# Six pipeline steps of the next tree issued beside the last leaf tiles of q and k, and overfull leaves in buffers of their own

## Chip, cores and metric

The kernel runs on one core of one Trainium2 chip. The metric is the device time of one execution in microseconds (us); lower is better. Before the change the median of 14 executions is 2463.23 us (2460.74 to 2474.45).

The engines are named as in the profile: PE (matrix multiply, with PEld its weight loads), DVE (vector), ACT (scalar, which also issues DMAs), POOL (GpSimd, which here issues all indirect DMAs) and SP (which only issues DMAs). Each runs its own instruction stream in order, and they meet through semaphores.

## What is computed

The input is 4 x 1024 tokens of 256 numbers. Three residual blocks follow one another: half of a fast-feedforward attention block, a 16-head attention block, and the feedforward block once more.

```python
x = x + 0.5 * ffn(layernorm(x), ...)
x = x + attention(layernorm(x), ...)
x = x + 0.5 * ffn(layernorm(x), ...)
```

Inside `ffn` there are four hard-routed trees, q, k, v and f. A tree walks 8 levels for each token (`node = 2*node + 1 + (logit > 0)`), arrives at one of 256 leaves, and applies that leaf's two small layers (256 to 16 and 16 to 256):

```python
h = act(einsum('bsd,bsdl->bsl', x, w1[leaf]) + b1[leaf])
return einsum('bsl,bsld->bsd', h, w2[leaf]) + b2[leaf]
```

q, k and v are trees over the same normalised rows, then `softmax(q k^T / 16) v` is added, and the f tree (gelu in place of relu) runs over the result.

## The kernel before, in words

**Leaf tiles.** The first five levels of a tree are one matrix product for all tokens; they give each token one of 32 blocks of eight leaves. Tokens are sorted by block into tiles of 128 rows, every tile belonging to one block. There are 48 tiles that are always computed and, where blocks fill badly, up to 15 more: `SPARE = (0, 48, 53, 58, NGRP)` (L294) cuts them into parts.

**The pipeline of a tree** is the generator `leaves` (L827). A tile passes five stages: `load` gathers its rows by an indirect DMA on POOL (L819), `turn` transposes them on PE (L844) and copies them on ACT (L846), `hidden` is the first layer and the last three levels (PE L866 and L873, DVE L882 to L897), `active` transposes that (PE L911, L912; ACT L920, L923), and `result` is the second layer (PE L931, L932), a copy (ACT L946) and a store to DRAM (SP L947). Step g of the loop runs the result of tile g-6, `hidden` of g-2, `turn` of g, `active` of g-4, and asks for the rows of g+4. So the 48 tiles take 54 steps, of which the first six fill the pipeline and the last six drain it. The rings of buffers: five for gathered rows, three each for most others. The first three tiles of k and v have rows of their own (`first_rows`, L1080).

**Beside the leaves.** `with_steps` (L1056) calls one step of each side generator after each step of the main one: the placement of the next tree's tokens (`placing`, about 42 steps, whose product `inv` the next gathers need and whose `gblk` names each tile's block), in the first `ffn` the building of the next tree's first layer from raw weights (`load_first`, 16 pieces, one every third step) and the keeping of this one in DRAM (`keep_first`). In the second `ffn` the first layer is loaded back in one DMA instead (`load_kept`, 4352 KB).

**Spare tiles.** After the 54 steps of a tree, `spare_leaves` (L809) runs the parts above 48 in three nested conditional blocks. The number of tiles used is loaded into a register of each engine (L797), and each engine branches by itself (L811). A skipped block must still bring the semaphores to the counts that it would have reached, so each engine waits at the branch for its own outstanding work: PE, DVE and ACT for theirs, POOL for its gathers and SP for the DMAs of the SP and ACT queues. Nothing outside a conditional block is mixed with what is inside, so the blocks also part the program.

**Order.** The leaves of q, k and v are not in an order written by hand: when the program is built, the instructions between two conditional blocks are put into an order for each engine by priority (program order) and by a plan of when each is ready. Instructions marked `keep_in_program_order` keep theirs.

**Between trees.** In the loop over q and k (L1176) the next tree's weights are asked for at the top: biases, second layer and, in the first `ffn`, raw weights, from the ACT queue. The tiles of v share their buffers with q's weights, so those loads wait for the last tile of q, spare ones included. Behind the loop v's leaves run beside `coming` (L1230), which gathers 24 finished k and q tiles from DRAM on POOL and transposes them for the scores (L1227), one every second step.

Of the kernel before, what the change touches and what calls it, by code (L numbers as in the profile page):

```python
# [77 lines left out]
def macaron_kernel(ctx: ExitStack, tc: tile.TileContext, a: dict, out: bass.AP):  # L78
# [223 lines left out]
    def split_b2(pool):  # L302

        n = NBLK // B2G * E
        rest = pool.tile([P, n], F32, name="b2_rest")
        part = [pool.tile([P, n], BF16, name=f"b2_part{s}") for s in range(3)]
        none = pool.tile([P, 3 * B2P // P], BF16, name="b2_none")
        nc.gpsimd.memset(none, 0.0)
        for f, nm in enumerate(FFFS):
            nc.scalar.dma_start(  # L310
                rest[f * NBLK : (f + 1) * NBLK].rearrange("p (q c) -> p q c", c=E),
                a[f"{nm}_b2"].rearrange("(q p) c -> p q c", p=NBLK),
            )
            nc.gpsimd.dma_start(
                b2i[f].rearrange("s n -> (s n)").rearrange("(p c) -> p c", p=P), none
            )
        for s in range(3):
            nc.gpsimd.tensor_copy(part[s], rest)
            for f in range(len(FFFS)):
                rows = b2i[f][s].rearrange("(r n) -> r n", r=B2G)[:, : EPB * B2W]  # L320
                nc.gpsimd.dma_start(
                    rows.rearrange("r (e w) -> r e w", e=EPB)[:, :, :n],
                    part[s][f * NBLK : (f + 1) * NBLK],
                )
            if s < 2:
                nc.gpsimd.tensor_sub(rest, rest, part[s])

# [467 lines left out]
    def tiles_used(gblk):  # L795
# [11 lines left out]
        return used  # L807

    def spare_leaves(used, *what):  # L809

# [216 lines left out]
    def ffn(first: bool, last: bool):  # L1027
# [6 lines left out]
        def stage(es, name, bufs, side="left"):  # L1034
            return es.enter_context(
                tc.tile_pool(name=name, bufs=bufs, side=side, reuse_waits="tile")
            )

        with ExitStack() as es:
# [31 lines left out]
            with ExitStack() as ws, banks(0, 8):  # L1071
                wp = stage(ws, "w", 1)

                fp = stage(ws, "first", 1)

                def tree(lp, f, got, *weights):
                    what = b1p[f], sel[f], own[f], inv[f], gblk[f], AF.Relu, None, got
                    return lp, f, *weights, *what

                def first_rows(f):  # L1080
# [3 lines left out]
                with ExitStack() as hs, ExitStack() as rs:  # L1084
                    hot = hots_of(stage(hs, "hots", 1), 3)
                    raw = stage(hs, "raw", 1) if first else None

# [84 lines left out]
                    wb = stage(rs, "w_k", 1, "right")  # L1172
                    lp = stage(hs, "leaves", 2)
                    pp = stage(hs, "place", 1)
                    got = {}
                    for f in range(2):  # L1176
                        what = tree(lp, f, got, w1, w2, b2s)
                        used = tiles_used(gblk[f])
# [19 lines left out]
                        else:  # L1198
                            tc.keep_in_program_order(load_kept(nc.scalar, f + 1, w1))
                            sides = ((1, second(10)),)  # L1200
                        with_steps(leaves(*what), (1, placing(pp, f + 1)[1]()), *sides)
                        (w2,) = coming_w2
                        got = first_rows(f + 1)
                        spare_leaves(used, *what)
                    if first:
# [3 lines left out]
                hold_rows()  # L1209
                lp = stage(ws, "leaves_v", 2)  # L1210
                early = stage(ws, "early", 2)
# [36 lines left out]

                what = tree(lp, 2, got, w1, w2, b2s)
                used = tiles_used(gblk[2])  # L1250
                sides = ((1, keep_first(2, w1, 4, 4, 4, 4)),) if first else ()
                with_steps(leaves(*what), (1, coming()), *sides)
                spare_leaves(used, *what)

# [661 lines left out]
```

## Time and profile before

| | us |
|---|---|
| median of 14 runs | 2463.23 |
| the profiled execution, its own time | 2469.78 |
| its span, first to last instruction | 2468.0 |
| leaf tiles of q, k, v in the first ffn, first transposes | 121.2, 228.9, 326.0 |
| leaf tiles of q, k, v in the second ffn, first transposes | 1737.3, 1844.8, 1945.8 |
| tiles of q, k, v in the first ffn | 48, 48, 53 |
| tiles of q, k, v in the second ffn | 53, 48, 48 |

The profiled execution lies 6.55 us above the median. Times in the profile are counted from the start of the span. A row of the timeline gives start, duration, engine, source line, operation, the tile it writes and reads, and in brackets how long the engine was idle before and what ended that; "issue" means that the engine waited for nothing that the profile shows. The granted clock (PEclk) is PE's clock as the throttle gave it, as a share of full speed.

### The profile page before, as it was taken

How to read it: one execution, taken by the hardware profiler on the slowest of the kernel's cores; microseconds unless marked ns; L12 is line 12 of the kernel's file. 1: busy time of each engine (PE TensorE's matmuls, PEld its weight loads, DVE VectorE, ACT ScalarE, POOL GpSimd, SP SyncE). 2: the span in 40 equal slices, each digit the busy share in tenths (PEclk: the TensorE clock that was granted, in tenths of full speed). 3: DMA queues.
4: the chain of work that ended last, by engine and by line, in shares of the span. 5: the costliest groups of instructions: out<-in, count | busy, mean ns of one | idle time of the engine just before them, and what ended most of it. 6: DMA issues, size and time to landing. Idle time of an engine off the chain costs nothing. (4 is left out here: it accounts for less than half of the span.)

```text
span 2468.0 us, 42918 instructions
## 1 busy us (share of the span) xinstructions
PE 2171.6 (88%) x13949; PEld 1391.3 (56%) x13949; DVE 1419.9 (58%) x4712; ACT 1076.4 (44%) x2870; POOL 814.0 (33%) x1045
## 2 busy tenths in 40 slices
PE   4588979999997889999999999995788889999794
PEld 2377867666666644434434444433677776666483
DVE  6676745333346766666676667746757553333475
ACT  3255546233323324555555555553455562332142
POOL 4554546332244521101100100001545563432553
PEclk8699989999998889999999999998899999999897
DMA  9687776343355400000000000008557564431655
GB/s 322 197 277 239 251 238 167 128 120 120 101 182 183 142 1 1 1 1 1 1 14 6 1 10 16 12 8 306 180 154 251 158 173 152 126 107 39 201 163 166
DMA packets 201876, 303.34 MB, mean 123 GB/s; under 512 B 25130, under 2 KB 174011, under 8 KB 197025
## 3 DMA queue, kind: packets, MB, share of 16 engines
q1 hardware_dynamic: 104080, 112.89, 14.1%
q0 software_dynamic: 35552, 91.87, 13.1%
q10 hardware_dynamic: 62000, 95.52, 11.3%
q8 instruction: 130, 2.13, 0.4%
q14 instruction: 114, 0.93, 0.1%
HBM read 182.88 MB, written 122.15 MB: 124 GB/s over the span
## 5 line engine op out<-in xcount | busy, mean ns | idle before, releaser
L1666 DVE TENSOR_REDUCE mxh<-big 128x1 f32<-128x512 f32 (+3 forms) x768 | 393.0, 552 | 194.1 <-PE big L1658 192.3
L1702 ACT ACTIVATE pTh<-big 128x512 f32<-128x512 f32 (+3 forms) x768 | 341.3, 491 | 288.9 <-PE big L1658 265.0
L1658 PE MATMUL big<-kTh,qTh 32*128 32x512 f32 (+3 forms) x1536 | 402.0, 538 | 1.5 <-ACT kTh L1639 1.4
L1694 PE MATMUL big<-qTh,kTh 32*128 32x512 f32 (+3 forms) x1536 | 400.7, 537 | 1.9 <-ACT pTh L1702 1.6
L846 ACT COPY xgT<-sm 128x256 f32<-128x256 f32 x399 | 148.6, 373 | 292.2 <-PE sm L844 258.9
L995 PE MATMUL two<-kT,qT 128*128 128x512 f32 x512 | 234.3, 602 | 9.7 <-issue 8.3
L1023 PE MATMUL sm<-vb,pT 128*128 128x256 f32 x1024 | 232.6, 380 | 0.0
L1694 PEld LDWEIGHTS big<-qTh,kTh 32*128 32x128 f32 x1536 | 143.5, 184 | 156.6 <-issue 127.0
L1023 PEld LDWEIGHTS sm<-vb,pT 128*128 128x128 f32 x1024 | 189.7, 190 | 24.6 <-issue 1.0
L844 PE MATMUL sm<-ident,xg 128*128 128x128 f32 x774 | 157.2, 287 | 41.2 <-DMA xg<-xs_f 11.9
L1003 DVE TENSOR_REDUCE mx<-two 128x1 f32<-128x1024 f32 x64 | 78.3, 1224 | 195.1 <-PE two L995 195.1
L882 DVE SCALAR_TENSOR_TENSOR went<-sm,sides 128x14 bf16<-128x14 f32 x399 | 67.9, 170 | 181.0 <-PE sm L873 171.9
L1713 PE MATMUL sm<-pTh,vpad 128*32 128x512 f32 (+3 forms) x1536 | 165.2, 501 | 0.0
L1658 PEld LDWEIGHTS big<-kTh,qTh 32*128 32x128 f32 x1536 | 146.4, 185 | 20.3 <-issue 14.1
L995 PEld LDWEIGHTS two<-kT,qT 128*128 128x128 f32 x512 | 93.7, 192 | 107.3 <-issue 104.0
L946 ACT COPY og<-sm 128x256 f32<-128x256 f32 x298 | 111.0, 373 | 90.2 <-DMA os_q<-og 21.3
L819 POOL DMA_INDIRECT xg<-rows_x,inv_q x101 | 101.5, 1005 | 112.2 <-PE sm L912 50.6
L937 POOL DMA_INDIRECT ytok<-og,tok x101 | 99.3, 983 | 80.5 <-DVE went L882 68.0
L420 POOL TENSOR_TENSOR acc<-acc,oh 128x32 bf16<-128x32 bf16 (+1 forms) x128 | 39.6, 310 | 253.0 <-DVE oh L418 221.9
L819 POOL DMA_INDIRECT xg<-rows_x,inv_k x90 | 91.9, 1021 | 89.8 <-PE sm L912 46.8
L897 DVE TENSOR_TENSOR hm<-sm,mask 128x128 f32<-128x128 f32 x399 | 115.2, 289 | 10.1
L920 ACT ACTIVATE hid<-sm 128x128 f32<-128x128 f32 x399 | 112.9, 283 | 10.6 <-PE sm L912 10.4
(371 smaller groups left out, 4417.2 us busy)
## 6 DMA issues: line engine op xcount, KB each, us to landing
xs_f<-zero ACTq DMA_DIRECT2D x14, 1028.0 KB
xg<-xs_f SPq DMA_DIRECT2D x101, 128.5 KB
os_q<-og SPq DMA_DIRECT2D x101, 128.0 KB
os_v<-og SPq DMA_DIRECT2D x101, 128.0 KB
os_k<-og SPq DMA_DIRECT2D x96, 128.0 KB
xn<-in_x SPq DMA_DIRECT2D x16, 512.0 KB
w_q<-in_q_w SPq DMA_DIRECT2D x2, 4096.0 KB
rows_x<-xn ACTq DMA_DIRECT2D x16, 512.0 KB
```

What stands on the lines that cost most here:

```text
L819: nc.gpsimd.indirect_dma_start(out=xg, out_offset=None, in_=rows_x, in_offset=bass.IndirectOffsetOnAxis(ap=inv[:, g : g + 1], axis=0),)
L844: nc.tensor.transpose(pa[:, c, :], xg[:, c * P : (c + 1) * P], ident)
L846: nc.scalar.copy(xT, pa)
L897: nc.vector.tensor_tensor(hm.rearrange("p (e l) -> p e l", l=LW), ph[:, :P].rearrange(split, l=LW), bc(mask[:, 0], 2, LW), ALU.mult,)
L920: nc.scalar.activation(hid, pt[:, 0], func)
L995: nc.tensor.matmul(ps[:, n0 : n0 + 512], qT[:, c, i * P : (i + 1) * P], kT[:, c, n0 : n0 + 512], start=(c == 0), stop=(c == KC - 1),)
L1023: nc.tensor.matmul(po, pT[:, j, :], vb[:, j, :], start=(j == 0), stop=(j == TPB - 1))
L1658: matmul = nc.tensor.matmul(ps[:, :n], qT[r : r + HPAD, hg, i * P : (i + 1) * P], kT[r : r + HPAD, hg, n0 : n0 + n], start=True, stop=True,)
L1666: nc.vector.tensor_reduce(maxima(b, hg)[:, i, c, u : u + 1], ps[:, :n], AX.X, ALU.max)
L1694: matmul = nc.tensor.matmul(ps[:, off:], kT[r : r + HPAD, hg, j * P : (j + 1) * P], qT[r : r + HPAD, hg, qb * QN + off : (qb + 1) * QN], s ...
L1702: nc.scalar.activation(pT[:, u, off:], ps[:, off:], AF.Exp, scale=1.0 / math.sqrt(HD))
L1713: nc.tensor.matmul(acc[r : r + HPAD, off:], vpads[b % 2][:, j, 4 * hg + 2 * pair + u, :], pTs[pair][:, u, off:], start=(j == 0), stop=(j = ...
```

## The change

The loop no longer makes a new `leaves` generator for each tree. One generator `main` is carried along. A side generator `head` waits for 44 steps, gathers the next tree's first rows, waits for four more, makes the next tree's generator and runs its first six steps; the next turn of the loop, or v's part, goes on from there with 48 steps left. The spare tiles come after these six steps, so in q and k they can't use the rings in which the next tree's tiles now wait: `Carved` cuts rings for them from the two 8 KB buffers for raw weights. These buffers now exist in the second `ffn` too, and the pool of leaf buffers is opened at the start of the `ffn` and kept through v. To make room, `split_b2` holds two of its three parts at a time and fills `b2i` from a zero buffer half as large.

```diff
-        part = [pool.tile([P, n], BF16, name=f"b2_part{s}") for s in range(3)]
-        none = pool.tile([P, 3 * B2P // P], BF16, name="b2_none")
+        none = pool.tile([P, 3 * B2P // P // 2], BF16, name="b2_none")
...
         for s in range(3):
-            nc.gpsimd.tensor_copy(part[s], rest)
+            part = pool.tile([P, n], BF16, name=f"b2_part{s}", tag="b2_part", bufs=2)
+            nc.gpsimd.tensor_copy(part, rest)
...
+    class Carved:
+
+        RINGS = {
+            "xg": (0, 0, 5, E), "hm": (0, 5 * E, 3, P), "hid": (0, 5 * E + 3 * P, 3, P),
+            "xgT": (1, 0, 3, E), "mask": (1, 3 * E, 4, B2R // 2),
+            "mT": (1, 3 * E + 2 * B2R, 3, P // 2),
+        }
+
+        def __init__(self, pool, raw):
+            self.pool, self.turn = pool, {}
+            self.homes = [
+                raw.tile([P, P * LW], F32, name=f"carved{i}", tag="raw", bufs=2)
+                for i in range(2)
+            ]
+
+        def tile(self, shape, dtype, name, tag, bufs=None):
+            if tag not in self.RINGS:
+                return self.pool.tile(shape, dtype, name=name, tag=tag, bufs=bufs)
+            home, at, n, width = self.RINGS[tag]
+            k = self.turn[tag] = (self.turn.get(tag, -1) + 1) % n
+            rows = self.homes[home][: shape[0], at + k * width : at + (k + 1) * width]
...
                 fp = stage(ws, "first", 1)
+                lp = stage(ws, "leaves", 2)
...
+                HEAD = 6
...
-                    raw = stage(hs, "raw", 1) if first else None
+                    raw = stage(hs, "raw", 1)
...
-                    lp = stage(hs, "leaves", 2)
                     pp = stage(hs, "place", 1)
-                    got = {}
+                    main = leaves(*tree(lp, 0, {}, w1, w2, b2s))
+
+                    def head(f, weights):
+
+                        nonlocal main
+                        for _ in range(SPARE[1] - PRE):
+                            yield
+                        rows = first_rows(f)
+                        for _ in range(PRE):
+                            yield
+                        main = leaves(*tree(lp, f, rows, *weights()))
+                        yield from islice(main, HEAD)
+
                     for f in range(2):
-                        what = tree(lp, f, got, w1, w2, b2s)
+                        spare = w1, w2, b2s
...
-                        with_steps(leaves(*what), (1, placing(pp, f + 1)[1]()), *sides)
+                        with_steps(
+                            main,
+                            (1, placing(pp, f + 1)[1]()),
+                            *sides,
+                            (1, head(f + 1, lambda: (w1, coming_w2[0], b2s))),
+                        )
                         (w2,) = coming_w2
-                        got = first_rows(f + 1)
-                        spare_leaves(used, *what)
+                        spare_leaves(used, *tree(Carved(lp, raw), f, {}, *spare))
...
-                lp = stage(ws, "leaves_v", 2)
...
-                what = tree(lp, 2, got, w1, w2, b2s)
                 used = tiles_used(gblk[2])
                 sides = ((1, keep_first(2, w1, 4, 4, 4, 4)),) if first else ()
-                with_steps(leaves(*what), (1, coming()), *sides)
-                spare_leaves(used, *what)
+                with_steps(main, (1, coming()), *sides)
+                spare_leaves(used, *tree(lp, 2, {}, w1, w2, b2s))
```

More of the change, by code (lines that the diff above doesn't have):

```diff
@@ L314, in split_b2 @@
             nc.gpsimd.dma_start(
-                b2i[f].rearrange("s n -> (s n)").rearrange("(p c) -> p c", p=P), none
+                b2i[f].rearrange("s n -> (s n)").rearrange("(p i c) -> p i c", p=P, i=2),
+                bc(none, 1, 2),
             )
         for s in range(3):
-            nc.gpsimd.tensor_copy(part[s], rest)
+            part = pool.tile([P, n], BF16, name=f"b2_part{s}", tag="b2_part", bufs=2)
+            nc.gpsimd.tensor_copy(part, rest)
             for f in range(len(FFFS)):
@@ L322, in split_b2 @@
                     rows.rearrange("r (e w) -> r e w", e=EPB)[:, :, :n],
-                    part[s][f * NBLK : (f + 1) * NBLK],
+                    part[f * NBLK : (f + 1) * NBLK],
                 )
             if s < 2:
-                nc.gpsimd.tensor_sub(rest, rest, part[s])
+                nc.gpsimd.tensor_sub(rest, rest, part)
     def clear(queue, rows):
@@ L807, in tiles_used @@
         return used
+    class Carved:
[16 more added lines that the diff above has]
+            rows = self.homes[home][: shape[0], at + k * width : at + (k + 1) * width]
+            if dtype != F32:
+                rows = rows.bitcast(dtype)
+            if len(shape) == 3:
+                rows = rows.rearrange("p (a b) -> p a b", b=shape[2])
+            return rows
     def spare_leaves(used, *what):
```

## The prediction

> **What bounds the kernel now.** I read the page first, then the timeline of PE around the four places where q hands over to k and k to v, then POOL, ACT and SP there, then the waits in v.
>
> ```profile
> span 2468.0 us, 42918 instructions
> PE 2171.6 (88%) x13949; PEld 1391.3 (56%) x13949; DVE 1419.9 (58%) x4712; ACT 1076.4 (44%) x2870; POOL 814.0 (33%) x1045
> ```
>
> PE is busy 88% of the span, so its gaps are what can be won. Inside the leaf tiles there are few:
>
> ```profile
> 1814.09 0.65 PE L931 MATMUL sm<-w_q,hid 128*128 x2
> ...
> 1815.60 0.65 PE L931 MATMUL sm<-w_q,hid 128*128 x2
> ...
> 223.81 0.28 PE L932 MATMUL sm<-b2s_q,mT 96*128 x1
> 228.86 0.66 PE L844 MATMUL sm<-ident,xf 128*128 128x128 f32 x2 [4.78 <-issue]
> ```
>
> A full step takes 1.51 us (first two rows). The last two rows are the hand-over of q to k in the first ffn: PE ends q, and for 4.78 us waits for nothing that the profile shows, while it jumps over the skipped spare block (the branches of L811 in PE's queue last up to 5.63 us). The other three gaps are 3.95 (322.1), 4.74 (1840.1, after q's five spare tiles) and 6.18 us (1939.6), on the mean 4.91. From the last full step of one tree to the first result of the next:
>
> ```profile
> 217.46:236.37 18.91, 12.02 (x78) 9.71 (x76) 8.36 (x42) 6.35 (x21) 7.70 (x11) 0.82 0.83 247
> 317.52:336.10 18.58, 11.58 (x68) 9.77 (x66) 5.46 (x24) 5.48 (x18) 2.45 (x4) 0.72 0.57 178
> 1822.76:1853.17 30.41, 21.15 (x130) 16.87 (x128) 12.30 (x60) 10.43 (x36) 5.06 (x7) 0.83 0.56 155
> 1935.10:1953.71 18.61, 11.78 (x66) 9.92 (x65) 5.54 (x24) 5.40 (x18) 9.06 (x10) 0.72 0.44 131
> ```
>
> The columns are the length, then busy time of PE, PEld, DVE, ACT and POOL, the granted clock, the DMA share and GB/s. I call these T1 to T4. In T1, T2 and T4 some 18.7 us pass for six steps of work, 6 x 1.51 = 9.06. Half of the bubble is drain and fill, half the jump.
>
> **The change, part by part.** Drain and fill become six full steps, 9.06 us. The jump stays: the branch still stands between six steps and the rest, and its code is still there: 4.91 us. The load of 16 block numbers into PE's registers moves into the full steps; where it stands between full steps now (292.1, 1911.8) it costs 1.21 and 0.52 us, so 0.87. And PE comes out of the jump slow:
>
> ```profile
> 229.00:233.00 4.00, 3.75 (x18) 3.11 (x19) 2.69 (x12) 1.12 (x3) 2.66 (x5) 0.51 1.10 311
> 1948.00:1953.00 5.00, 5.00 (x26) 4.76 (x25) 2.91 (x13) 1.30 (x4) 3.87 (x4) 0.50 0.60 197
> ```
>
> Four us at 0.51 lose 4 x 0.49 = 2.0 us of full steps, where before they hid in a half-empty fill. So a clean hand-over takes 9.06 + 0.87 + 4.91 + 2.0 = 16.8 us.
>
> [...]
>
> T1: 18.91 becomes 16.8, a gain of 2.1. But the carved rings take both raw buffers at the branch, so the first two raw_v loads, now issued at 194.6 and 216.7, move behind it on ACT's queue (0.34 us each to issue), ahead of the copies for PE, and must wait until POOL too has passed its branch. PE's first turn of raw_v comes two slow steps after the jump, some 6 us, about what 1 MB takes to land; I charge 0.6. T1 gains 1.5; bounds: a gain of 8.5 if the jump shrinks to almost nothing, a loss of 3 if raw_v comes late.
>
> T2: here the new tree's first layer is built by 16 pieces, every third step, and k's generator has only 48 steps left, so the last piece now falls into k's drain. v's first layer waits for it; drain (4.6) plus two pieces (0.7 each), four fill steps of about 1.2, jump, registers and slow clock make 4.6 + 1.4 + 4.8 + 4.9 + 0.9 + 2.0 = 18.6, as long as now. What T2 does win is a later stall (2.86 us at 341.8, v's gathers queued on POOL behind gathers of k's results, which waited for SP's branch at 334.0). v is bound by POOL:
>
> ```profile
> 2022.42 0.95 POOL L819 DMA_INDIRECT xg<-rows_x,inv_v  x1 [0.30 <-PE sm L912]
> 2023.67 0.95 POOL L982 DMA_INDIRECT y_k<-os_k,slot_k  x1 [0.30 <-PE sm L873]
> 2024.92 0.95 POOL L982 DMA_INDIRECT y_k<-os_k,slot_k  x1 [0.30 <-PE sm L932]
> ```
>
> One gather each 1.25 us, 72 for v's 48 tiles and 24 fetched ones. Seven of v's tiles are gathered before the branches now, ten afterwards: 3 x 1.25 = 3.75. I take 3.5; bounds a gain of 7 and a loss of 1.
>
> T4 has no build: 18.61 becomes 16.8, 1.8, of which POOL leaves, by the same count, about 1.2; bounds 3.5 and a loss of 1.5.
>
> T3 holds q's spare tiles and v's weights:
>
> ```profile
> 1840.46 0.94 POOL L819 DMA_INDIRECT xg<-rows_x,inv_k  x1 [17.53 <-PEq L811]
> 1847.01 0.44 ACTq L788 DMA_DIRECT2D w_v<-w1d_v  x1
> 1853.01 0.94 POOL L819 DMA_INDIRECT xg<-rows_x,inv_k  x1 [6.60 <-PE sm L873]
> 1863.33 0.66 PE L844 MATMUL sm<-ident,xg 128*128 128x128 f32 x2 [5.85 <-DMA xg<-rows_x,inv_k]
> ```
>
> k's gathers wait for the end of q's spare tiles, then run into the 4352 KB load of w_v (issued at 1847.0), and PE stands 5.85 us for tile 8. In the new order q's drain and k's fill end at 1822.8 + 9.9 = 1832.7. The spare gathers, now queued behind k's ten on POOL, come some 3 us late (a gather lands 2.7 to 4.8 us after its issue where no weights load); five spare tiles then take 10 us as now (1830.3 to 1840.1), to 1845.5, 5.4 later than now. So the weight load also starts 5.4 later and again holds a gather up, to about 1868, but at tile 12 instead of 8. Tile 12 is turned at 1872.2 now. I take 3.5; bounds a gain of 5 and a loss of 3.
>
> **A cost behind.** v's generator also has only 48 steps left, and `coming` needs 53. The 24th fetch is called after v's last step, and its buffer is free only once the 21st is turned: the fetch, 3 us to land and the turn may stand at v's end. Between 0 (the plan draws it forward) and 4 us in each ffn; I take 1.5 each, 3.0, since the planner drew POOL's gathers ahead elsewhere (k's first rows at 197.6, before q's last).
>
> **At nothing.** The third b2 part waits for the four DMAs of the first, issued at 34.4 to 36.8, while its copy runs at 49.9: covered by 13 us of POOL's work; without that cover the accumulation of routes (L420), queued behind it, would be late. The zero buffer's memset, 1.53 us, is halved, while POOL is idle for 24 us afterwards. q's first gathers no longer share memory with the placement; they start at 114.1, when the index lies ready at 113.3: 0 to 1 us, counted as 0. The ten gathers issued early go through POOL past nothing that is waited for, as POOL stands idle 5 to 17 us at each hand-over.
>
> **Sum.** -1.5 - 3.5 - 3.5 - 1.2 + 3.0 = -6.7. The profiled execution would go from 2469.78 to 2463.1, the median, 6.55 below it, from 2463.2 to 2456.5; I say **2456**. Its own range, not all terms at one end, is 2448 to 2461. No change is 2458.3 to 2468.2 (0.2%).
>
> **The rivals.** *Half a change.* `head` needs 54 steps and k has 48, so for v the six steps are called after k's drain. If the plan leaves them there, T2 and T4 gain nothing: -1.5 - 3.5 + 3.0 = -2.0, 2461. For it: program order is the priority. Against: the plan does draw work forward (the gathers at 197.6), and k's drain leaves PE idle slots.
>
> *POOL starves PE.* The slower side, one mechanism. POOL must pass its own skip before k's tile 10 is gathered:
>
> ```profile
> 314.51 0.94 POOL L819 DMA_INDIRECT xg<-rows_x,inv_v  x1 [5.05 <-DMA xg<-rows_x,inv_k]
> ```
>
> That skip waited 5.05 us here, 6.45 at 1935 and from 1821.7 to 1830.7 with the spare tiles, always hidden because PE drained. Now POOL reaches it only after gathering tile 9, about 8.5 us behind the last full step. At 5.5 us for the skip and 4 to land, tile 10 is there at 18; PE comes out of the jump at 14.8 and needs it four tiles, 8 us, later. If the skip takes 9 and the landing 7 (as at 227.6 under a weight load), it comes at 25.5, 2.5 late, with another 1 to 2 us of slow clock. The mechanism decides from 14 us for both together. At 4 us in each of four hand-overs, and the tails at their dearer end (+5): -6.7 + 16 + 5 = +14, 2477; without the tails 2472.
>
> *A short jump.* If PE found its code, T1 to T4 would gain 4 x (4.5 + 2.0) = 26 more: 2430. Neither target nor distance changes, so little speaks for it.
>
> **How the numbers follow.** Forecast 0.55 (faster 0.46, within 0.2% 0.08, slower 0.01); half a change 0.21 (0.03, 0.15, 0.03); starved 0.18 (0, 0.01, 0.17); short jump 0.06 (faster). Faster 0.55, same 0.24, slower 0.21. The range reaches to 2446 (half of the short jump's cases and the best bounds of T1 and T3) and to 2470, where the starved case begins.
>
> **What would show it.** PE: full steps of 1.51 us straight across the last tiles of q and k, then one gap of 4 to 6 us, then slow matmuls of 0.42 for 0.27 us. POOL: ten gathers of the next tree before the skip. PE's wait for gathered rows in T3 still there, four tiles later. Turns of y_k after v's last result would show the tail. Wrong: PE waiting after the jump for gathered rows or for raw_v; drain and fill of T2 and T4 still one after the other.

## The result, and the profile after

The changed kernel takes 2496.63 us (median of 6 runs, 2487.96 to 2498.29) against 2463.23 (28 runs): ratio 1.0123, 95% interval 1.0107 to 1.0139. It is 33 us slower, where 7 us less were forecast. The profiled execution took 2494.32 us, 2.3 below its median; that of before lay 6.55 above its own. So the two traces differ by 24.5 us only, and some 9 us of the medians' difference are in neither.

The top of the page, to be held against the first fence of the prediction:

```profile
span 2492.5 us, 42895 instructions
PE 2174.1 (87%) x13949; PEld 1389.8 (56%) x13949; DVE 1416.8 (57%) x4712; ACT 1073.2 (43%) x2870; POOL 814.2 (33%) x1045
```

PE does the same 13,949 matmuls in 2.5 us more of busy time and idles 22 us longer. The hand-overs themselves, from the last result of one tree to the first of the next (T1 to T4; the third has q's spare tiles in it), and four microseconds behind the last jump, with the columns as before (length; busy PE, PEld, DVE, ACT, POOL; granted clock; DMA share; GB/s):

```profile
219.84:225.55 5.71, 1.42 (x11) 1.09 (x11) 1.18 (x6) 1.17 (x4) 1.56 (x2) 1.00 0.52 146
329.84:341.60 11.76, 5.47 (x43) 4.66 (x42) 4.11 (x18) 3.12 (x10) 1.89 (x2) 0.86 0.69 222
1842.77:1865.19 22.42, 12.64 (x74) 9.82 (x73) 6.54 (x30) 6.83 (x23) 6.66 (x7) 0.77 0.47 87
1960.11:1971.70 11.59, 5.02 (x38) 4.21 (x37) 3.41 (x17) 3.17 (x11) 1.89 (x2) 0.93 0.33 103
1971.00:1975.00 4.00, 4.00 (x16) 3.18 (x16) 1.23 (x5) 0.97 (x3) 1.70 (x2) 0.50 0.20 59
```

So the next tree's first result follows the last one's sooner. But only at q's hand-overs do the six steps stand beside the last tiles. In T1 k's first turns lie among q's last results; in T2 v's first turn comes behind k's last result, and in T4 too (1959.94 after 1959.31):

```profile
215.89 0.38 PE L872 MATMUL sm<-ident,xf 128*128 128x128 f32 x2
...
219.08 0.65 PE L959 MATMUL sm<-w_q,hid 128*128 x2
...
329.03 0.70 PE L959 MATMUL sm<-w_k,hid 128*128 x2
...
330.12 0.60 PE L872 MATMUL sm<-ident,xf 128*128 128x128 f32 x4
```

`head` needs 54 steps and k's generator has 48 left, and the plan did not draw v's steps forward: drain and fill still follow one another there. What T2 and T4 gain is a fill ahead of the jump, at a granted clock of 1.00 (4.7 and 5.3 us to the jump), in place of one behind it, at 0.53 to 0.54 (10.1 and 7.9 us to v's first result).

The time is lost elsewhere. The timeline of PE shows where (start, duration, what is computed, idle time ahead and what ended it):

```profile
225.05 0.67 PE L959 MATMUL sm<-w_k,hid 128*128 x2 [4.29 <-issue]
...
340.62 1.19 PE L959 MATMUL sm<-w_v,hid 128*128 x2 [5.78 <-SPq L839]
...
1749.73 0.66 PE L872 MATMUL sm<-ident,xg 128*128 128x128 f32 x2 [9.22 <-DMA xg<-rows_x,inv_q]
...
1851.01 0.66 PE L872 MATMUL sm<-ident,carved 128*128 128x128 f32 x2 [6.84 <-DMA carved<-rows_x,inv_q]
...
1887.14 1.22 PE L959 MATMUL sm<-w_k,hid 128*128 x2 [10.06 <-ACT hid L948]
...
1970.72 1.19 PE L959 MATMUL sm<-w_v,hid 128*128 x2 [5.52 <-issue]
...
2053.94 0.41 PE L1272 MATMUL sm<-ident,y_k 128*128 128x128 f32 x2 [2.31 <-DMA y_k<-os_k,slot_k]
...
2062.00 4.57 PE L1023 MATMUL two<-kT,qT 128*128 128x512 f32 x6 [5.67 <-issue]
```

The first, second and sixth row are the jump over the skipped block, about as long as before (4.78, 3.95 and 6.18 us there). The third is new: q's second tile in the second `ffn` waits 9.22 us for its rows. The fourth is a spare tile of q that waits for its own. The fifth is the old wait beside the load of w_v, nearly twice as long (10.06 us after 5.85) and now through ACT and the stores. The seventh is the tail: a fetched k row is still to be turned behind v's last result (2051.1), and the eighth is the gap ahead of the scores. ACT's queue has the cause of two of them; first the changed kernel, then the kernel before:

```profile
1734.53 1.27 ACTq L998 DMA_DIRECT2D b2s_k<-b2i_k  x3
1738.49 0.35 ACTq L789 DMA_DIRECT2D w_k<-w1d_k  x1
...
1869.00 0.43 ACTq L789 DMA_DIRECT2D w_v<-w1d_v  x1
...
1886.26 0.37 ACT L974 COPY og<-sm 128x256 f32<-128x256 f32 x1 [12.66 <-DMA os_k<-og]
```

```profile
1708.67 1.60 ACTq L970 DMA_DIRECT2D b2s_k<-b2i_k  x3
1710.32 0.43 ACTq L788 DMA_DIRECT2D w_k<-w1d_k  x1
```

The 4352 KB of w_k were asked for 24 us ahead of q's first gather (1734.41); now they are asked for 1.7 us behind it (1736.80), and the five gathers issued from 1738.2 to 1743.2 take 11.4 to 14.5 us to land, in place of 2.7 to 3.5 for those issued from 1735.8 to 1740.8 before. w_v is asked for at 1869.0, lands at 1885.8, and the stores of k's results issued at 1870 to 1872 land at 1886.2 to 1886.9, so that ACT stands 12.66 us for a result buffer and PE behind it.

The same two traces by stage. "q48" is the 48th result of q, "k24" the 24th of k, and so on; each number is the difference of two such times.

| stage | before | after | difference |
|---|---|---|---|
| start to q1, first `ffn` | 130.8 | 133.2 | +2.5 |
| q1 to k24 (T1 in it) | 150.4 | 148.5 | -1.9 |
| k24 to v48 (T2) | 141.7 | 139.0 | -2.6 |
| v48 to the first scores | 17.3 | 21.9 | +4.6 |
| scores to the end of f | 393.8 | 394.6 | +0.7 |
| end of f to q12, second `ffn` | 933.0 | 942.4 | +9.4 |
| q12 to q48 | 62.9 | 63.3 | +0.5 |
| q48 to k24 (T3) | 73.6 | 80.7 | +7.2 |
| k24 to v48 (T4) | 130.3 | 127.4 | -2.8 |
| v48 to the first scores | 4.7 | 10.9 | +6.2 |
| scores to the end of f | 394.8 | 395.8 | +1.0 |

Three hand-overs gain, 7.3 together. Five other places lose 29.9. The row of T2 is itself a sum: from k24 to k48 the first `ffn` takes 47.9 us in place of 40.7, and from k48 to v48 9.8 less. So from q's first to k's last result, T1 and all of k, it takes 196.6 us in place of 191.3.

### The profile page after: what moved, and what is told of

Its sections match the earlier page's. It is cut to its first block, busy times and chain, and to the rows that moved or that the text cites. A ratio compares the mean times of both kernels' runs of the same rounds, so it can differ in the third digit from the quotient of the medians.

```text
span 2492.5 us, 42895 instructions
## 1 busy us (share of the span) xinstructions
PE 2174.1 (87%) x13949; PEld 1389.8 (56%) x13949; DVE 1416.8 (57%) x4712; ACT 1073.2 (43%) x2870; POOL 814.2 (33%) x1045
## 5 line engine op out<-in xcount | busy, mean ns | idle before, releaser
L1031 DVE TENSOR_REDUCE mx<-two 128x1 f32<-128x1024 f32 x64 | 78.3, 1224 | 197.0 <-PE two L1023 197.0
L910 DVE SCALAR_TENSOR_TENSOR went<-sm,sides 128x14 bf16<-128x14 f32 x399 | 67.7, 170 | 191.3 <-PE sm L901 174.2
L925 DVE TENSOR_TENSOR hm<-sm,mask 128x128 f32<-128x128 f32 x394 | 113.8, 289 | 10.1
L948 ACT ACTIVATE hid<-sm 128x128 f32<-128x128 f32 x394 | 112.0, 284 | 10.4 <-PE sm L940 10.2
```

What stands on the lines that cost most here:

```text
L925: nc.vector.tensor_tensor(hm.rearrange("p (e l) -> p e l", l=LW), ph[:, :P].rearrange(split, l=LW), bc(mask[:, 0], 2, LW), ALU.mult,)
L948: nc.scalar.activation(hid, pt[:, 0], func)
```

## The experiments

My theory after this reading: the bubbles were cover. In them weights were loaded, POOL passed its own branch, and stores drained; without them the same work stands beside running tiles. And two edits that I had counted at nothing (memory, zero buffer) have a price of their own. The rivals stand in the expectations.

Twelve of the fifteen runs were made on chips where the kernel before takes 2570 to 2576 us in place of 2463 to 2467 (v's tiles, f and the scores are slower there, see the end); ratios are to the kernel before on the same chip, and stages are compared between kernels run on like chips.

**b2_alone**: the changed `split_b2` in the kernel before.

> The kernel before with the changed split_b2 alone (two parts at a time, zero buffer half as large). Theory 'small pieces': the zero fill in pieces of half the size takes the DMA engines longer at the very start and delays the input rows; q's first transpose comes at about 123.2 us in place of 121.2, and the whole is 2 us slower, about 2465. Rival 'chance': the 2 us at the start belong to the one profiled execution; 121.2 and 2463 again.

Ratio 1.0018 (0.9996 to 1.0040), 2574.3 against 2569.75. The first transpose of input rows and the zero fills on POOL, in this kernel and then before:

```profile
3.96 0.72 POOL L313 DMA_DIRECT2D b2i_q<-b_none  x1 [0.24 <-POOL b_k L725]
...
5.70 1.09 POOL L313 DMA_DIRECT2D b2i_f<-b_none  x1
...
32.13 2.16 PE L391 MATMUL sm<-ident,xn 128*128 128x128 f32 x8 [7.85 <-ACT xn L1142]
```

```profile
4.67 0.57 POOL L314 DMA_DIRECT2D b2i_q<-b_none  x1 [0.24 <-POOL b_k L724]
...
6.29 0.54 POOL L314 DMA_DIRECT2D b2i_f<-b_none  x1
...
30.18 2.17 PE L390 MATMUL sm<-ident,xn 128*128 128x128 f32 x8 [7.85 <-ACT xn L1141]
```

The fills start 0.6 to 0.7 us earlier, and the rows still come 1.95 us later. Over all traces of this study, the row on PE comes at 30.2 to 31.4 in the four with pieces of the old size and at 31.9 to 33.8 in the thirteen with halves: 2.4 us on the mean, of which 1.5 are left at q's first transpose (121.3 against 122.8, with single traces from 120.2 to 122.8 and from 120.5 to 124.3). The total alone could not show it.

**carved_alone, no_head, own_rings_2nd**: which edit moved w_k's load.

The first is made from the kernel before (for q and k; `Carved` is added), the others from the changed kernel, in this order:

```diff
-  raw = stage(hs, "raw", 1) if first else None
+  raw = stage(hs, "raw", 1)
...
-  spare_leaves(used, *what)
+  spare_leaves(used, Carved(lp, raw), f, *what[2:-1], {})
```

```diff
-  HEAD = 6
+  HEAD = 0
```

```diff
-  raw = stage(hs, "raw", 1)
+  raw = stage(hs, "raw", 1) if first else None
...
   pp = stage(hs, "place", 1)
+  spares = raw if first else stage(hs, "carved", 1)
...
-  spare_leaves(used, *tree(Carved(lp, raw), f, {}, *spare))
+  spare_leaves(used, *tree(Carved(lp, spares), f, {}, *spare))
```

> The kernel before with the rings for spare tiles cut from the raw buffers, which therefore exist in the second ffn too; no head, no other change. Theory 'memory': in the second ffn the placement of q now lies where k's first layer is to go, so that the 4352 KB load of w_k is issued at about 1735 in place of 1710 and runs beside q's first gathers: PE stands about 9 us, and the whole takes 10 us more; in the first ffn the raw_v loads move behind the branch, 0 to 3 us more: 2473 to 2477. Rival 'place of the leaf buffers': it is the early pool of leaf buffers (not here) that pushes the placement there; then w_k is still issued at 1710 and the whole takes 2463 to 2466.

> The changed kernel with HEAD = 0: nothing of the next tree's pipeline is run ahead, all else as changed. Theory 'lost cover': the 10 us at the start of the second ffn's q and the 2 us at the start stay, the stalls of k beside the weight loads shrink to what they were before (5.85 us in the second ffn), and v has its 54 steps again, so that the tails of some 5 and 6 us go: 2475 to 2479. Rival 'the head pays, the rest costs': without it the hand-overs are as long as before and everything else stays, so it is slower than the changed kernel's 2496.6: 2500 to 2508.

> The changed kernel, but in the second ffn the rings for spare tiles lie in a pool that is opened after q's placement; there are no raw buffers below the placement there. Theory 'memory': w_k is loaded at about 1710 again, the stall of 9.2 us at q's second tile goes, and the time falls by about 10, to 2486 to 2488. Rival 'place of the leaf buffers': their early pool alone still pushes the placement into w_k's place: no change, 2495 to 2498.

Ratios 1.0030 (1.0009 to 1.0050), 1.0098 (1.0070 to 1.0126) and 1.0100 (1.0075 to 1.0125). ACT's w_k load in the first and the third, then PE's second tile with ACT's load in no_head, then the second tile in own_rings_2nd (four kernels and views, one line or two of each):

```profile
1756.69 0.36 ACTq L788 DMA_DIRECT2D w_k<-w1d_k  x1
```

```profile
1767.28 0.35 ACTq L789 DMA_DIRECT2D w_k<-w1d_k  x1
```

```profile
1784.08 0.66 PE L872 MATMUL sm<-ident,xg 128*128 128x128 f32 x2 [9.28 <-DMA xg<-rows_x,inv_q]
```

```profile
1772.80 0.35 ACTq L789 DMA_DIRECT2D w_k<-w1d_k  x1
```

```profile
1795.06 0.66 PE L872 MATMUL sm<-ident,xg 128*128 128x128 f32 x2 [1.07 <-DMA xg<-rows_x,inv_q]
```

In carved_alone the load comes 27.6 us ahead of q's first transpose (1784.24; in b2_alone it is issued at 1757.5, so nothing moved), in own_rings_2nd 26.0, in no_head 1.3. So neither edit alone does it: the raw buffers below the placement (carved_alone has them) and the early pool of leaf buffers (own_rings_2nd has it) together push q's placement into w_k's memory, and my expectation for carved_alone, which blamed the raw buffers, fell. With the load late, q's first result comes 19.7 to 20.7 us behind its first transpose (7 traces); with it early, or in pieces, 9.7 to 10.8 (10 traces). That is the 9.4 us of the table, shown from both sides. The attention ahead of it, which no edit touches, takes 807 to 821 us in the seventeen traces, so the stage is better taken from q's last routing product to q12: 57.3 to 60.1 us with the load early, 67.3 to 68.1 with it late. In the totals it can't be told: own_rings_2nd was to be at 1.009 to 1.010 and is at 1.0100, but the changed kernel itself, run again, is at 1.0108. no_head was to be at 1.005 to 1.0065; at 1.0098 it has most of the loss without any step run ahead, so the edits around the head cost more than the head; I can account for the 9 us, the 1.5 of the start and some 4 us at the spare tiles (14.8 us from q48 to the last of them, 10.6 in b2_alone), and not for the rest. What was expected of its stages came: the tails go (4.9 us from v48 to the scores), and beside the load of w_v PE waits 4.12 us, where the changed kernel waits 10.06.

**after_again, pieces**: the load of w_v beside k.

```diff
-  tc.keep_in_program_order(load_kept(nc.scalar, f + 1, w1))
-  sides = ((1, second(10)),)
+  sides = ((1, second(10)), (1, kept_pieces(f + 1, w1, 4, 8, 8, 8)))
```

`kept_pieces` is `keep_first` with source and destination exchanged.

> The changed kernel once more, so that what follows has its like on the same chip. If the stalls found in its first trace are its own, they are here again at the same places: 9 us at q's second tile in the second ffn (w_k's load beside the first gathers), some 10 us in k of the second ffn, 2 to 4 us three times in k of the first, and 10 us in place of 4 between v's last result and the scores. The ratio to the kernel before is about 1.012. Rival 'chance': the places change from execution to execution.

> The changed kernel, but in the second ffn the first layers of k and v (4352 KB each) are read back in four DMAs of a quarter, issued at steps 4, 12, 20 and 28 of the tree before, in place of one. Theory 'lost cover' (a large load beside running tiles holds up their gathers and their stores): with pieces of 4 us between steps the 9 us at q's second tile go, and of the 10 us in k at most 3 stay; 14 to 17 us less than the changed kernel. Rival 'order' (the tiles of k wait for the late spare tiles and the branch, not for the load): the 10 us in k stay, only the 9 in q go: 8 to 10 less.

after_again has ratio 1.0108 (1.0079 to 1.0138) and the stalls at the same places; PE and ACT there, then PE and ACT's queue with pieces:

```profile
1941.09 1.22 PE L959 MATMUL sm<-w_k,hid 128*128 x2 [10.19 <-ACT hid L948]
```

```profile
1940.21 0.37 ACT L974 COPY og<-sm 128x256 f32<-128x256 f32 x1 [13.03 <-DMA os_k<-og]
```

```profile
1966.96 1.22 PE L969 MATMUL sm<-w_k,hid 128*128 x2 [3.19 <-ACT hid L958]
```

```profile
1943.88 0.34 ACTq L800 DMA_DIRECT2D w_v<-w1d_v  x1
...
1958.23 7.65 ACTq L800 DMA_DIRECT2D w_v<-w1d_v  x1
```

The 10 us shrink to 3.2, as 'lost cover' said, and the 9 at q's second tile go. But those come back at once: from q1 to q12 this kernel takes 29.0 us, every other one 19.9 to 22.2, and from the last routing product to q12 67.3, as with the late load. And pieces has ratio 1.0125 (1.0096 to 1.0155): not faster, where 14 to 17 us less were expected. By stages of the second `ffn`:

| | q12 to q48 | q48 to k24 | k24 to k48 |
|---|---|---|---|
| no head here: before, best_again; b2_alone, head_T2 | 62.9, 62.1; 67.8, 66.7 | 73.6, 74.7; 72.9, 73.8 | 36.0, 36.0; 45.0, 40.3 |
| head, one load: changed kernel; after_again, own_rings_2nd | 63.3; 65.6, 66.9 | 80.7; 82.9, 81.4 | 36.1; 41.4, 40.3 |
| head, pieces: pieces, mended, mended_v | 73.0, 67.0, 67.7 | 69.8, 75.6, 74.7 | 43.0, 44.2, 46.7 |

With a head the single load costs 7 to 10 us from q48 to k24, and the pieces give most of them back; no_head, whose wait at the load is short, has 79.4 there, 4.2 us of it by slower spare tiles than in b2_alone. So it is the load beside a full pipeline that costs in this stage. Then the later pieces take 2 to 6 us between k24 and k48, and w_k's pieces 6 to 7 more between q12 and q48. Wherever these runs put the bytes, they cost something.

**plain_q_rows, tail_short, fetch_first**: the way from k's last result to the scores.

In this order, each from the changed kernel; in the second and third the first two yields of `coming` go as well:

```diff
-  y = fetch(pool, f, t, slot[f], bufs, tag)
+  if f == 0:
+      y = pool.tile([P, E], F32, name="y_q", tag="y_", bufs=bufs)
+      nc.sync.dma_start(y, osrt[0][t * P : (t + 1) * P, :])
+  else:
+      y = fetch(pool, f, t, slot[f], bufs, tag)
```

```diff
   next(live[-1])
   yield
-  yield
+  if b == 0:
+      yield
```

```diff
+  fetches = coming()
+  for _ in range(5):
+      next(fetches)
-  with_steps(main, (1, coming()), *sides)
+  with_steps(main, (1, fetches), *sides)
```

> The changed kernel with the 8 fetches of finished q rows beside v made by plain DMAs on SP's queue in place of gathers on POOL (the rows are then not in the order of the tokens, so that this part of the result is left out). Theory 'POOL bound' (v and what follows it last as long as POOL's 62 gathers at 1.25 us): in the second ffn the way from v's first result to the first scores (90.3 us in the first trace) becomes about 10 us shorter, 80. Rival 'steps' (the last fetch comes late because v's generator has 48 steps for 53): the tail of some 6 us stays as it is and the way shrinks by no more than 2.

> The changed kernel with the 24 fetches beside v packed into 45 steps: the first at once, the first eight one every second step and the later sixteen one every step. Theory 'POOL bound': POOL has as many gathers as before, so at most 2 to 3 us of each tail go, and v's own tiles wait for rows instead; 0 to 4 us less than the changed kernel. Rival 'steps': all turns of fetched rows lie ahead of v's last result, and both tails go, 10 us less.

> The changed kernel with the first three fetches of finished k rows placed ahead of v's remaining steps, so that on POOL they stand before the gather of v's next tile, which waits 7 to 8 us for PE to come out of its jump. Theory 'POOL bound and idle at the branch': three of 62 gathers move into that idle time, and from k's last result to the scores the second ffn takes 3 to 5 us less (changed kernel: 101.9 in its first trace, 119.1 when it was run again), the first ffn 2 to 4 less; 5 to 9 us in all. Rival 'steps': no gain, since the last fetches come as late as before or the turns of the fetched rows only move.

Ratios: tail_short 1.0140 (1.0076 to 1.0205), fetch_first 1.0095 (1.0058 to 1.0132). The total of plain_q_rows says nothing, since with other rows from the first `ffn` the second has fewer spare tiles; its v has 48 tiles all the same. From k's last result to the scores, second `ffn`, with v's part from first to last result and the part behind it:

| | chip like the first | | | slower chips | | |
|---|---|---|---|---|---|---|
| | whole | v | behind v | whole | v | behind v |
| before; b2_alone | 98.7 | 79.7 | 4.4 | 116.8 | 99.0 | 4.7 |
| changed; after_again | 101.9 | 79.7 | 10.6 | 119.1 | 94.0 | 12.0 |
| tail_short | | | | 120.4 | 103.2 | 4.2 |
| fetch_first | 101.2 | 85.1 | 4.6 | | | |
| plain_q_rows | | | | 107.5 | 84.0 | 10.7 |

The tail can be moved into v (tail_short, fetch_first), and then v is as much longer: that the steps cost time, as 'steps' has it, is out. Eight gathers less save 11.6 us, 1.45 each (expected 1.25 each): the number of POOL's gathers sets this stage. But 'steps' is right as to the place: with eight gathers less the tail stays as long (10.7), and POOL idles up to 2.92 us ahead of the last fetches, waiting for PE's turns. fetch_first was to gain 3 to 5 us and gained 0.7 (the first `ffn` nothing: 113.0 after 112.9), because POOL does not stand behind the gather of the next tile, as I thought, but at its own branch, and no fetch can come ahead of that. POOL in fetch_first, in the changed kernel and before:

```profile
1962.50 0.94 POOL L847 DMA_INDIRECT xg<-rows_x,inv_v  x1 [0.30 <-DVE mask L917]
1971.03 0.94 POOL L1010 DMA_INDIRECT y_k<-os_k,slot_k  x1 [7.59 <-issue]
```

```profile
1964.85 0.95 POOL L847 DMA_INDIRECT xg<-rows_x,inv_v  x1 [0.30 <-DVE mask L917]
1972.99 0.94 POOL L847 DMA_INDIRECT xg<-rows_x,inv_v  x1 [7.20 <-PE sm L960]
1974.24 0.95 POOL L1010 DMA_INDIRECT y_k<-os_k,slot_k  x1 [0.31 <-issue]
```

```profile
1927.80 0.95 POOL L819 DMA_INDIRECT xg<-rows_x,inv_k  x1 [0.30 <-PE sm L873]
1935.20 0.94 POOL L819 DMA_INDIRECT xg<-rows_x,inv_v  x1 [6.45 <-issue]
...
1946.91 0.94 POOL L982 DMA_INDIRECT y_k<-os_k,slot_k  x1 [7.02 <-PE sm L844]
```

Before, POOL is through its branch 4.4 us ahead of k's last result (1939.6) and makes the first fetch 7.3 us behind it, with 65 gathers to do from there. In the changed kernel it is through 12.9 us behind k's last result (1960.1), the first fetch comes 14.1 behind it, and 61 gathers are left: 6.8 us later, against 4.7 us saved by four gathers less (78.1 us from the first fetch to the last in place of 82.8). With the 1.1 us that the end takes longer, that is the 3.2 us by which the whole way grew. PE's drain had hidden POOL's branch.

**mended, mended_v, no_branch_T1**: T1 and the weights of v in the first `ffn`.

mended is own_rings_2nd with pieces for v alone and the first edit below; mended_v has the second in its place; no_branch_T1 is the changed kernel with the third.

```diff
-  drain(second(0))
   sides = (
+      (1, second(20)),
```

```diff
+      (1, second(20 if f else 0)),
```

```diff
-  spare_leaves(used, *tree(Carved(lp, raw), f, {}, *spare))
+  if f or not first:
+      spare_leaves(used, *tree(Carved(lp, raw), f, {}, *spare))
```

> The changed kernel with three covers given back, each in a stage of its own: in the second ffn no raw buffers under q's placement (rings for spare tiles in a later pool), and v's first layer read back in four pieces at steps 4, 12, 20 and 28 of k; in the first ffn the second layers of k and v (4096 KB each) asked for at step 20 of the tree before in place of step 0. Theory 'lost cover': the 9 us at q's second tile go; k in the second ffn, 94.9 to 101.3 us from its first to its last result in the runs so far, becomes about 91; q to k and k in the first ffn, 196.6 and 210.5 together, become 8 to 12 less, since SP's stores no longer wait for the load of w_v; what stays is the longer way from v to the scores. All in all 22 to 30 less than the changed kernel, ratio to before 1.000 to 1.003. Rival 'late raw weights' for the first ffn (it is the raw_v loads held until the branch that cost, not the load of w_v): there no more than 3 less, ratio 1.003 to 1.006.

> The run with the covers given back once more, but the second layer is asked for later (step 20) only for v, in k of the first ffn; k's is asked for at step 0 of q again. Theory 'load of w_v': the load of w_v holds SP's stores and so ACT and PE in k of the first ffn; k there, 104.3 to 110.8 us in the changed kernel and 102.9 with both layers later, is 100 to 103 again, while q, 105.4 with both later, falls back to 97 to 100; q to k and k together 198 to 202 against 205.9 to 210.5. Rival 'too much for the DMA queues whatever the order' (raw_v, w_v, the kept layer, gathers and stores all within k): both together stay at 205 to 210.

> The changed kernel without the conditional block behind q's last tile in the first ffn (no spare tile is needed there with these inputs; the part that would compute one is left out). So PE has no jump there, and the raw_v loads are held by no ring for spare tiles. Theory 'held raw weights': the jump (4.3 us) and the slow clock behind it (2 us) go, and with raw_v loaded during q's last tiles as before the change, k's stalls go too; from q's first to k's last result 186 to 194 in place of 205.9 to 210.5, that is 12 to 24 less. Rival 'too much for the DMA queues whatever the order': the raw loads are the same bytes in the same 100 us, PE only waits elsewhere; 4 to 7 less, 199 to 206.

Ratios 1.0093 (1.0064 to 1.0122; 1.000 to 1.003 was expected, 1.003 to 1.006 by the rival), 1.0076 (1.0056 to 1.0096) and 1.0085 (1.0036 to 1.0134). From q's first to k's last result the first two took 208.4 and 205.7 us, the changed kernel and its variants on such chips 205.9 to 210.5: theory 'load of w_v' falls as to the sum, though from q48 to k24 it is right (54.6 and 57.4 in place of 62.0 to 62.6). What is moved there comes back, in q with mended (q12 to q48 78.3 in place of 69 to 73), ahead of q's first result with mended_v (w_k is asked for 0.7 us behind q's first transpose there, and q1 comes at 140.9 in place of 132.5 to 134.5) and along the rest. In the second `ffn` the 9 us at q's second tile go in both, but k takes 96.0 and 99.1 us, where about 91 was expected. So 'lost cover' explains single stalls; it does not yield a kernel with heads everywhere that is as fast as before. Without the branch, 189.4 against 196.6 and 197.3 on like chips: 7 to 8 less, the jump (4.3 to 5.0), the 2 us of slow clock and hardly more. So held raw weights are not what costs. The rival, some DMA excess whatever the order, is left but not shown; I have not tested it by taking bytes away.

**head_T2, head_T2_zero, best_again**: a head at one hand-over only.

head_T2 is made from the changed kernel; head_T2_zero and best_again, which are the same kernel, have the second edit in `split_b2` too (and one fill of the old shape).

```diff
-  raw = stage(hs, "raw", 1)
+  raw = stage(hs, "raw", 1) if first else None
-  yield from islice(main, HEAD)
+  yield from islice(main, HEAD if first and f == 2 else 0)
-  spare_leaves(used, *tree(Carved(lp, raw), f, {}, *spare))
+  spare_leaves(used, *tree(Carved(lp, raw) if first and f else lp, f, {}, *spare))
```

```diff
-  none = pool.tile([P, 3 * B2P // P // 2], BF16, name="b2_none")
+  none = pool.tile([P, n], BF16, name="b2_none", tag="b2_part", bufs=2)[:, : 3 * B2P // P]
```

> Six steps of the next tree are run ahead at one hand-over only, from k to v in the first ffn, where the raw buffers are no longer needed by anybody; at the three others the kernel is as before (spare tiles in the common rings, no raw buffers in the second ffn). The smaller zero buffer stays. Theory 'lost cover': only here is no load waiting to be covered; from k's last to v's last result the first ffn takes 4 to 7 us less, everything else is as before but for the 2 us of the smaller zero buffer: 2 to 5 less than before, ratio 0.998 to 1.000. Rival 'a head costs wherever it stands' (jump, clock, POOL held at the branch): no gain there, and 2 to 6 slower than before, ratio 1.001 to 1.003.

> Six steps ahead at the hand-over from k to v in the first ffn alone, and a zero buffer of the old size again (it lies in the ring of the two parts). Theory 'small pieces': the 2 us at the start come back; first transpose of q at about 121 in place of 123; the whole 4 to 7 us less than before, ratio 0.997 to 0.9985. Rival 'order of the queues' (the 2 us come from the changed order of the DMA issues, not from the size of the pieces): first transpose at 123 again, ratio 0.998 to 1.000.

> The kernel with six steps ahead at the hand-over from k to v of the first ffn alone and the zero buffer of the old size, once more, since its first comparison (ratio 0.9979) was made where the kernel before takes 2576 us. If the gain is that of the hand-over, some 4 to 6 us wherever it is run, the ratio is 0.9975 to 0.9985 again; rival 'chance': within 0.999 to 1.001.

Ratios 0.9985 (0.9970 to 1.0001), 0.9979 (0.9966 to 0.9993) and, where the kernel before takes 2466.68 us, 0.9983 (0.9968 to 0.9997): 2462.2 us. This version beats both kernels, by 4.5 us at the chip of the first comparison's kind and 7.8 (medians) at the other. With the old zero buffer q's first transpose comes at 120.2 in head_T2_zero, as 'small pieces' said, but at 122.8 in best_again, the same kernel, so these two leave 'order of the queues' open. PE in best_again, one of v's first turns, k's last result, and the jump:

```profile
324.67 0.38 PE L871 MATMUL sm<-ident,xf 128*128 128x128 f32 x2
...
327.86 0.65 PE L958 MATMUL sm<-w_k,hid 128*128 x2
...
333.92 0.85 PE L958 MATMUL sm<-w_v,hid 128*128 x2 [4.39 <-issue]
```

The jump is there as everywhere (4.39 us). But no raw weight waits to be loaded behind this branch, and k24 to v48 takes 131.3 us against 141.7 before: 10.4 less, of which the tail behind v48 gives back 4.6 (21.9 against 17.3, as in the changed kernel). The same hand-over won 2.6 in the changed kernel, and two things differ: here k has had no head and keeps its 54 steps, so that v's steps do stand beside k's last tiles and POOL's first fetch comes 10.6 us behind k's last result in place of 14.1; and k24 to k48 takes 43.4 us in place of 47.9, v's steps included. No run separates the two, and none gives T4 a head beside a k of 54 steps.

## Why the prediction was wrong

Forecast was a sum of -6.7 us; the traces show +24.5.

- **The drain and fill** were right at T1 and T3 only. At T2 and T4 they still follow one another, which the prediction named as a sign of being wrong.
- **The jump, the slow clock** were right. At T1, T2 and T4 the jump stays (4.29, 5.78 and 5.52 us; 4.91 was taken), and the clock behind it is 0.50 to 0.59 for 4 us; only behind T3's spare tiles PE now waits 1.04 us where it was 4.74.
- **T1** (-1.5 forecast) is -1.9 from q1 to k24 in the first pair of traces, and -1.4 in fetch_first on a like chip. On the slower chips it costs 1.5 to 6.5, and over 5 in carved_alone without any step ahead. The raw_v loads did move behind the branch (194.6 and 216.7 before, 227.5 and 227.9 after), as foreseen. But the stage must not end at k24: up to k48 it is +5.3, beyond my bound of 3. I priced the late raw_v by PE's first turn of it alone; what costs in the rest of k stays open.
- **T2** (-3.5) is -2.6 by the table, -9.8 from k48 on; **T4** (-1.2) is -2.8. T4 has that without the overlap from which I took it, by the fill at full clock. And for both I counted POOL's gain by the gathers made ahead of the branch, and not the time at which POOL is at work again. I wrote that the ten early gathers pass nothing that is waited for, "as POOL stands idle 5 to 17 us at each hand-over"; part of that idle time was the branch itself, and it moved with them to behind k's last result, 6.8 us late against 4.7 saved.
- **The tail** (+1.5 in each `ffn`, bounds 0 to 4) is +4.6 and +6.2, beyond my bound. I had its place and its chain right: the last fetch comes behind v's last result (2052.4 after 2051.1). What was wrong is the price, and the hope that the plan draws it forward: POOL makes one gather each 1.30 us from the first fetch to the last, and drawing the fetches forward only lengthens v.
- **T3** (-3.5) is +7.2: the step that failed most. I let the weight load's stall keep its 5.85 us and only come at a later tile. Ahead of the change k's stage behind the load was still filling, with few stores and results; with the pipeline full, the load also holds the stores (12.66 us on ACT), and the stall is 10.06, on top of the spare tiles' late gathers (a wait of 6.84, where I had them 3 us late). A store of 128 KB, 1.7 us elsewhere in k (1886.66 to 1888.34), takes 16.1 beside the load (1870.03 to 1886.16); the load comes in rows of 34,816 bytes and a store in rows of 1,024. In the trace the load's 128 packets take 1.41 us each on the mean and those of the three stores beside it 0.05, and 302 of these 384 start only from 1883 on, while the load's first parts land at 1883.2; why they start so late there, the trace doesn't show.
- **At nothing** failed twice. The load of w_k (+9.4) is not in the prediction at all: I looked at what q's gathers share with the placement, and not at what the placement, pushed up by two pools, shares with k's weights. The smaller zero buffer was counted by POOL's idle time; it keeps the DMA engines longer (its packets take 92 us of their time together, against 73 to 80 before and in best_again) and makes q late (+2.5 in this pair, 1.5 on the mean of all).
- **The rivals**: 'half a change', to which I gave 0.21, is what happened at T2 and T4, though not its price: it had them gain nothing, and it has none of the losses. 'A short jump' is out: no run shows the 4.5 us that it would have saved at each hand-over, the jumps stay at 4.29 to 5.78 us. 'POOL starves PE' gave the nearest time (2472 to 2477) by a mechanism that isn't there: after a jump PE waits more than 1.2 us for gathered rows only in T3, and those are the spare tiles' own. What POOL's branch delays is not the next tile but the fetches a whole stage later.

## What to carry to other kernels

A bubble is cover: before filling it, list what runs in it on every other engine and queue (weight loads, stores draining, another engine's own branch) and price each of them beside a full pipeline, where here a load hurt through stores and result buffers too (a store of 128 KB took 16.1 us beside it, ACT stood 12.66 and PE 10.06). A pool that is opened earlier moves the addresses of all that is opened above it (two such pools together brought w_k's load from 24 us ahead of q's first gather to 1.7 us behind it); ask of each late load whose memory it now waits for. Count the steps as well: a head that needs 54 steps finds no place beside a tree that has given six away. The one hand-over without such work, and with all its 54 steps, paid alone (10.4 us from k24 to v48, 4.5 in the whole), where all four together lost 33.

## What I had not expected of the hardware

- A load held a store by its semaphore, too. In k of the first `ffn` SP issues a store at 244.94 and the next at 255.18; the semaphore that it waits for in between is that of w_v's load, issued by ACT at 229.64 and landed at 255.12. In this trace both queues take their semaphores from the same eight in turn (100 and 102 to 108), and the load and the store at 255.18 have the same one, 104.
- Beside zero fills of the same bytes in rows of half the length (320 packets of 5,058 bytes and 64 of 1,686 in the trace, in place of 256 of 6,744) the first transpose of input rows comes 2.4 us later, on the mean of these traces.
- The chips of these runs differ by 4%: the kernel before takes 2463 to 2467 us on some and 2570 to 2576 on others. On the slower ones v takes 94 to 99 us for 48 tiles in place of 80, at the same granted clock (1.00 in 40 us from the middle of v in b2_alone and before). PE of b2_alone there:

```profile
2061.40 0.70 PE L932 MATMUL sm<-w_v,hid 128*128 x2 [1.03 <-issue]
...
2065.91 0.48 PE L932 MATMUL sm<-w_v,hid 128*128 x1 [1.05 <-issue]
```

Every second tile PE stands for about 1 us, and ACT, DVE and POOL, which wait for PE's earlier results, all start again within 0.3 us of one another (2060.70 to 2060.97), though PE's last matmul ahead of the pause started at 2060.1. Why PE's signals come late there, the trace doesn't show.
